# Scores with the keys in the partitions, maxima from a pass of their own, and a rotary turn in sums and differences

## The chip, the cores and the metric

The kernel runs on one core of a Trainium2 chip. The metric is device time in microseconds, the median of some runs. Beside the runs there is one profiled execution; its trace gives the durations used below. The engines are PE (matrix products, with PEld for loading weights), DVE, ACT and POOL (elementwise work), and SP, which here only issues DMAs.

## What is computed

A transformer block on x with 2048 rows and 1024 columns, all in float32:

```
h  = layernorm(x)
q, k, v = h Wq, h Wk, h Wv          # 16 heads of 64
q, k = rotary(q), rotary(k)         # t*cos + swapped(t)*sin, neighbours (0,1), (2,3), ... swapped, no sign
a  = softmax(mask(q k^T) / 8) v     # causal
x  = x + layernorm(a Wo)
x  = x + layernorm((silu(g Wg) * (g Wu)) Wd)   # g = layernorm(x); Wg, Wu, Wd from 4-bit codes and scales
```

## The kernel before

**Precision.** A float32 value is kept as a high part (rounded to the matmul's type fp32r) and a low part, the rest. A product of two such values is three matmuls (`mm3`, lines 225 to 227: high x high, high x low, low x high). ACT writes the high part, and DVE (or POOL) subtracts it for the low part.

**Stages.** Rows of x are normalized and transposed (`plan_rows`); q, k and v are projected for pairs of heads m and column groups c of 512 rows (`plan_qkv`), and written to DRAM as high and low parts (qs, ks, vs). Attention works in 64 blocks (head h, group J of 512 query rows). Then the attention rows are projected with Wo and normalized (five of the sixteen row tiles in `plan_project`, the other eleven in `attended`, `project`, `residual`), and the feed-forward part follows (gate and up for 22 column tiles, then a down projection in seven products).

**The order of the work.** All of the first part, until the end of attention and the first five row tiles, is written down as steps: an engine, a cost in microseconds, what it comes after, which buffers (`Room`) it takes, and a place `at` at which it is wanted. `Plan.order` replays the steps greedily: at each point it takes the step that could start first by these costs, the earlier place first among equals, on five in-order engines with limited buffers. The instructions are issued in that order. A chunk's values are wanted `LATE = 5` places after the scores of its block; a block (h, J) takes 4J + 4 places, and the 64 blocks 640. Loads are wanted `AHEAD = 8` places before. What follows the last query load in the program (the eleven row tiles, the feed-forward part) is ordered by a scheduler of the framework.

**A block of attention.** `plan_scores` makes scores with the queries in the partitions: for each of four tiles of 128 queries and each group of up to 512 keys, two matmuls into a bank S (line 322), DVE's maximum with the mask added on the diagonal (327, 329), and ACT's exponential with a running sum (334). When two query tiles are done, small operations on DVE and ACT (362 to 384) combine maxima and sums, and POOL scales each tile of probabilities by its factor (395). `plan_weighted` then takes chunks of 128 keys: PE transposes up to four 128 x 128 tiles of probabilities into a bank T (411), ACT and DVE split them into two parts (419, 422), and two matmuls with V add to a bank O (414). V holds its high and low parts side by side, 128 columns; at the end ACT copies one half and DVE adds the other (430, 431), and one DMA stores the block's result (attd). Matmuls on the diagonal are 512, 384, 256 and 128 wide. In all there are 640 score tiles, 640 chunks and 2176 transposes.

**Rotary.** After its projection, a tile of q or k is copied by ACT out of its bank (580), DVE makes a copy with neighbours swapped (612) and multiplies by the cosines (613), POOL multiplies the swapped copy by the sines and adds (614, 615), and ACT and DVE split the sum (616, 620).

**Buffers.** SBUF is cut into slots by size: 7 "hd" and 6 "pa" of 8 KB per partition, 4 "w", 4 "xc", 5 "f4" of 4 KB, 3 "pw", 4 "t2" of 2 KB and so on. The eight PSUM banks are F (1, projections), S (3, scores), T (3, transposes) and O (1).

Of the kernel before, what the change touches and what calls it, by code (L numbers as in the profile page):

```python
# [33 lines left out]
LATE = 5  # L34
# [6 lines left out]
EXPS = {512: 0.68, 384: 0.57, 256: 0.46, 128: 0.36}  # L41
CASTS = {512: 0.475, 384: 0.37, 256: 0.262, 128: 0.15}
PAIRED = {512: 0.602, 384: 0.468, 256: 0.334, 128: 0.202}
SCALES = {512: 0.668, 384: 0.562, 256: 0.45, 128: 0.347}
# [8 lines left out]
WO_AT = 26  # L53
PROJECT_AT = 36
PROJECT_STEP = 9
BATCH = 2
STEP = 4
FIRST = (0, 1, 2, 3)
# [18 lines left out]
class Room:  # L77
    def __init__(self, tag, make):
        self.tag, self.make, self.left, self.tile, self.open = tag, make, 0, None, False

# [14 lines left out]
class Plan:  # L95
# [4 lines left out]
    def add(self, engine, busy, lag, emit, after=(), rooms=(), at=0.0, port=False):  # L100
        step = Step(engine, busy, lag, emit, after, rooms, at, port)
        step.index = len(self.steps)
        self.steps.append(step)
        for a in step.after:
            a.next.append(step)
        for r in rooms:
            r.left += 1
        return step

    def order(self):  # L110
# [14 lines left out]
        while len(done) < len(self.steps):  # L125
            best = None
            for e, waiting in ready.items():
                for step in waiting:
                    t = max(step.ready, clock[e], wire - BACKLOG if e == "SP" else 0.0, port if step.port else 0.0)
                    for r in step.rooms:  # L130
                        if not r.open:
                            if queues[r.tag][-1] is not r or not self.free[r.tag]:
                                break
                            t = max(t, min(self.free[r.tag]))
                    else:
                        key = (t, step.at, step.index)
                        if best is None or key < best[0]:
                            best = key, step
# [3 lines left out]
            for r in step.rooms:  # L142
                if not r.open:
                    r.open = True
                    queues[r.tag].pop()
                    self.free[r.tag].remove(min(self.free[r.tag]))
# [9 lines left out]
            for r in step.rooms:  # L156
                r.left -= 1
                held[r] = max(held.get(r, 0.0), end + 0.05)
                if not r.left:
                    self.free[r.tag].append(held[r])  # L160
# [10 lines left out]
def block_kernel(ctx, tc, x, wq, wk, wv, wo, gu_codes, gu_scales, d_codes, d_scales, cos_sin, out):  # L171
# [12 lines left out]
    BANKS = {"F": 1, "S": 3, "T": 3, "O": 1}  # L184
    BANK_ORDER = ("F", "S", "S", "S", "T", "T", "T", "O")
# [21 lines left out]
    V.tensor_copy(mask_b, mask_f)  # L207
    nhalf = const.tile([P, 1], F32, name="nhalf")
# [68 lines left out]
    attd = [dram.tile([E, 512], F32, tag=f"at{c}", name=f"at{c}") for c in range(NC)]  # L277
# [11 lines left out]
    plan = Plan({"S": 3, "T": 3, "F": 1, "O": 1} | {t: SLOTS[t][0] for t in ("hd", "w", "xc", "pa", "pb", "f4", "pw", "t2", "ol")} | {"stats": 6, "ln": 6})  # L289
    kept, wrooms, xrooms, x_kept, shared, at_kept, wo_rooms = {}, {}, {}, {}, {}, {c: [] for c in range(NC)}, []  # L290

    def room(tag, shape, dtype, name):
        return Room(tag, lambda: slot(tag, shape, dtype, name))
# [10 lines left out]
    def plan_scores(J, q, half, k, q_in, k_in, start):  # L304
        nh = J + 1
        at = start
        prob = [room("pa", [P, 4, 512], F32, "prob") for _ in range(nh)]
        scaled, made = {}, {}
        stats = None
        for j in range(4):  # L310
            w = (4 * J + j + 1) * P
            if j % BATCH == 0:
                stats = Room("stats", lambda: [small.tile([P, BATCH, 4], F32, tag=n, name=n)[:, :, :nh] for n in ("mxs", "sums")])
            for i in range(nh):
# [4 lines left out]
                def score(b=b, e=e, s=s, j=j):  # L319
                    o = s()[:, : e - b]  # L320
                    for a in range(2):
                        T.matmul(o, lhsT=q()[:, half, a, j * P : (j + 1) * P], rhs=k()[:, b:e], start=a == 0, stop=a == 1)  # L322

                def top(b=b, e=e, s=s, j=j, i=i, diag=e == w, stats=stats):
                    o, mx = s()[:, : e - b], stats()[0][:, j % BATCH, i : i + 1]
# [5 lines left out]
                def power(b=b, e=e, s=s, j=j, i=i, diag=e == w, stats=stats):  # L331
                    mxs, sums = stats()
                    mx = mxs[:, j % BATCH, i : i + 1]
                    A.activation(  # L334
                        prob[i]()[:, j, : e - b],
                        s()[:, : e - b],
                        AF.Exp,
                        bias=mx,
                        scale=-1.0 if diag else 1.0,
                        accum_out=sums[:, j % BATCH, i : i + 1],  # L340
                    )

                x = on("PE", 2 * ROW[n], score, [q_in, k_in[i]], (s, q, k), at)
                y = on("DVE", PAIRED[n], top, [x], (s, stats), at, 0.055 if e == w else 0.0)
                z = on("ACT", EXPS[n], power, [y], (s, stats, prob[i]), at)
                made[j, i] = y, z
            if j % BATCH < BATCH - 1:
                continue
            rows = range(j - BATCH + 1, j + 1)
            tops = [made[jj, i][0] for jj in rows for i in range(nh)]  # L350
            sums_in = [made[jj, i][1] for jj in rows for i in range(nh)]
            got = {}

            def little(n, shape, got=got):
                got[n] = small.tile(shape, F32, tag=n, name=n)
                return got[n]

            if nh == 1:

                def invert(stats=stats, little=little, got=got):  # L360
                    got["rc"] = little("rc", [P, BATCH, 4])[:, :, :1]
                    V.reciprocal(got["rc"], stats()[1])

                last = on("DVE", 0.075, invert, sums_in, (stats,), at)
            else:

                def spread(stats=stats, little=little, got=got):
                    mxs = stats()[0]
                    nm = little("nm", [P, BATCH, 1])
                    V.tensor_reduce(nm, mxs, AX.X, ALU.min)  # L370
                    got["cf"] = little("cf", [P, BATCH, 4])[:, :, :nh]
                    V.tensor_tensor(got["cf"], mxs, nm.to_broadcast([P, BATCH, nh]), ALU.subtract)

                def weigh(got=got):
                    A.activation(got["cf"], got["cf"], AF.Exp, scale=-1.0)

                def total(stats=stats, little=little, got=got):
                    sums, cf = stats()[1], got["cf"]
                    sm = little("sm", [P, BATCH, 1])
                    V.tensor_tensor(sums, sums, cf, ALU.mult)  # L380
                    V.tensor_reduce(sm, sums, AX.X, ALU.add)
                    V.reciprocal(sm, sm)
                    got["rc"] = little("rc", [P, BATCH, 4])[:, :, :nh]
                    V.tensor_tensor(got["rc"], cf, sm.to_broadcast([P, BATCH, nh]), ALU.mult)  # L384

                first = on("DVE", 0.276, spread, tops, (stats,), at, port=True)
                second = on("ACT", 0.1, weigh, [first], (stats,), at)
                last = on("DVE", 0.671, total, [second] + sums_in, (stats,), at, port=True)
            for i in range(nh):
                for jj in rows:  # L390
                    n = min(512, (4 * J + jj + 1) * P - i * 512)

                    def scale(i=i, jj=jj, n=n, got=got):
                        p = prob[i]()[:, jj, :n]
                        G.tensor_scalar(p, p, got["rc"][:, jj % BATCH, i : i + 1], 0.0, ALU.mult, ALU.add)  # L395

                    scaled[i, jj] = on("POOL", SCALES[n], scale, [last, made[jj, i][1]], (prob[i], stats), at)
        return prob, scaled

    def plan_weighted(h, J, prob, scaled, v, v_in, start, pace):  # L400
        o, nk, chain = bank_room("O", "o"), 4 * J + 4, None
        for kb in range(nk):
# [3 lines left out]
            at = start + LATE + kb * pace  # L406
            pt, pw, pr = bank_room("T", "pt"), room("pw", [P, 2, 512], FR, "pw"), prob[kb // 4]

            def turned(kb=kb, j0=j0, pt=pt, pr=pr):
                for j in range(j0, 4):  # L410
                    T.transpose(pt()[:, j * P : (j + 1) * P], pr()[:, j, kb % 4 * P : (kb % 4 + 1) * P], ident)  # L411

            def times(a, kb=kb, cs=cs, pw=pw):
                T.matmul(  # L414
                    o()[:, cs], lhsT=v()[:, kb, :], rhs=pw()[:, a, cs], start=kb == 0 and a == 0, stop=kb == nk - 1 and a == 1
                )

            def rounded(cs=cs, pw=pw, pt=pt):
                A.copy(pw()[:, 0, cs], pt()[:, cs])  # L419

            def rest(cs=cs, pw=pw, pt=pt):
                V.tensor_tensor(pw()[:, 1, cs], pt()[:, cs], f32(pw()[:, 0, cs]), ALU.subtract)  # L422

            x = on("PE", (4 - j0) * TURN, turned, [scaled[kb // 4, j] for j in range(j0, 4)], (pt, pr), at)
# [727 lines left out]
```

## Time and profile before

| what | value |
|---|---|
| median of three runs | 2930.93 us (2929.71 to 2931.02) |
| profiled execution | 2933.72 us |
| its span, first to last instruction | 2931.9 us |
| granted clock of PE | 0.998 |
| PE, DVE, ACT, POOL busy | 99%, 70%, 58%, 33% of the span |
| DMA | 534.96 MB, 182 GB/s in the mean |

The page gives, for the profiled execution: busy times; the span in 40 slices with the busy tenths of each engine; DMA queues; the chain of work that ended last, followed back from the end; groups of instructions by source line, with their count, busy time, mean duration and the idle time of the engine before them; DMA issues with their time to landing. The trace behind it answers for single lines, tiles or stretches of time. In the trace, attention's first scores (line 322) start in the stretch from 75 to 150 us, and its last products with V (line 414) end in that from 1425 to 1500 us.

| stretch, us | PE busy, us | DVE | ACT | POOL | DMA share |
|---|---|---|---|---|---|
| 225 to 300 | 74.91 | 59.53 | 53.32 | 27.86 | 0.60 |
| 1050 to 1125 | 73.16 | 64.98 | 58.96 | 32.44 | 0.51 |
| 1275 to 1350 | 71.63 | 51.92 | 54.61 | 43.75 | 0.55 |
| 1500 to 1575 | 75.00 | 42.13 | 39.49 | 21.82 | 0.59 |
| 1800 to 1875 | 75.00 | 59.12 | 46.77 | 22.00 | 0.46 |

### The profile page before, as it was taken

Reading aid. Unit: us, or ns where it says so; the run is one execution under the profiler, and the core shown is the slowest. Engines: PE = TensorE matmul, PEld = TensorE weight load, DVE = VectorE, ACT = ScalarE, POOL = GpSimd, SP = SyncE. Lnnn points to the kernel's source line nnn. Section 1 sums busy time; section 2 is a strip of 40 time slices with the busy share of each in tenths; the row PEclk is TensorE's granted clock in tenths of the full one; section 3 lists DMA queues with packets and bytes.
Section 4 is the critical chain, followed back from the end, with each engine's and each line's share of the span. In section 5 each row is a group of like instructions: output and inputs, shape, how many; then the busy total and the mean of one; then the engine's idle time right before and its main releaser. Section 6 shows DMA issues by size and latency. Waiting matters only on the chain.

```text
span 2931.9 us, 42504 instructions
## 1 busy us (share of the span) xinstructions
PE 2888.4 (99%) x14192; PEld 2396.7 (82%) x14192; DVE 2050.5 (70%) x4167; ACT 1696.6 (58%) x3573; POOL 963.1 (33%) x1055
## 2 busy tenths in 40 slices
PE   8999999999999999999999999999999999999998
PEld 7878888888888888878787888888888888888887
DVE  7577887887878788777666766668766668443347
ACT  5366776676767677775556555556545546422234
POOL 5343444444434443554331221223222124000034
PEclk9999999999999999999999999999999999999999
DMA  9785676764858548573465443444443446644446
GB/s 325 270 243 207 186 224 216 234 195 151 256 181 223 201 138 262 168 229 117 148 219 169 149 136 118 137 137 155 136 136 120 133 137 204 233 141 150 147 140 226
DMA packets 271196, 534.96 MB, mean 182 GB/s; under 512 B 22912, under 2 KB 113024, under 8 KB 255104
## 3 DMA queue, kind: packets, MB, share of 16 engines
q1 hardware_dynamic: 270976, 532.24, 56.8%
q8 instruction: 112, 1.84, 0.3%
q14 instruction: 108, 0.88, 0.1%
HBM read 370.93 MB, written 161.22 MB: 182 GB/s over the span
## 4 chain that ended last, share of the span: by engine, by line
PE 91%; DVE 2%; ACT 2%; DMA 2%; issue 1%; POOL 1%; SPq 1%; POOLq 0%; DVEq 0%; ACTq 0%
PE bk L226 14%; PE bk L227 14%; PE bk L225 14%; PE o L414 8%; PE s L322 8%; PE pt L411 7%; PE qkv L225 6%; PE qkv L227 6%; PE qkv L226 6%; PE pj L658 2%; PE pj L789 1%; PE pj L787 1%; PE pj L788 1%; ACT prob L334 1%; PE pt L515 1%
## 5 line engine op out<-in xcount | busy, mean ns | idle before, releaser
L395 POOL TENSOR_SCALAR prob<-prob,rc 128x512 f32<-128x512 f32 (+3 forms) x640 | 398.9, 646 | 517.9 <-DVE rc L384 350.9
L225 PE MATMUL bk<-x,wt 128*128 128x512 f32 x1376 | 534.0, 390 | 0.8 <-ACT x L231 0.5
L227 PE MATMUL bk<-x,wt 128*128 128x512 f32 x1376 | 534.3, 390 | 0.0
L226 PE MATMUL bk<-x,wt 128*128 128x512 f32 x1376 | 534.2, 390 | 0.0
L334 ACT ACTIVATE prob<-s,mxs 128x512 f32<-128x512 f32 (+3 forms) x640 | 402.6, 631 | 146.1 <-DVE mxs L329 87.0
L422 DVE TENSOR_TENSOR pw<-pt,pw 128x512 fp32r<-128x512 f32 (+3 forms) x640 | 377.3, 605 | 96.9 <-ACT pw L419 91.9
L419 ACT CAST pw<-pt 128x512 fp32r<-128x512 f32 (+3 forms) x640 | 325.9, 528 | 159.8 <-PE pt L411 147.8
L846 ACT ACTIVATE ln<-cs,bias 128x512 f32<-128x512 f32 x520 | 354.5, 718 | 94.2 <-DVE cs L839 28.2
L414 PE MATMUL o<-pw,v 128*128 128x512 f32 (+3 forms) x1280 | 402.6, 381 | 5.4 <-ACT pw L419 3.0
L322 PE MATMUL s<-k,q 128*128 128x512 f32 (+3 forms) x1280 | 368.8, 380 | 8.0 <-ACT prob L334 6.2
L411 PE MATMUL pt<-ident,prob 128*128 128x128 f32 x2176 | 325.8, 273 | 1.8 <-DVE pw L422 1.8
L411 PEld LDWEIGHTS pt<-ident,prob 128*128 128x128 f32 x2176 | 264.3, 140 | 54.8 <-DVE pw L422 3.4
L225 PEld LDWEIGHTS bk<-x,wt 128*128 128x128 f32 x1376 | 258.5, 188 | 55.1 <-ACT x L231 0.8
L227 PEld LDWEIGHTS bk<-x,wt 128*128 128x128 f32 x1376 | 258.7, 188 | 54.1 <-DVE wt L232 0.3
L226 PEld LDWEIGHTS bk<-x,wt 128*128 128x128 f32 x1376 | 258.8, 188 | 53.5
L329 DVE TENSOR_REDUCE mxs<-s 128x1 f32<-128x512 f32 x384 | 262.1, 684 | 53.8 <-PE s L322 51.8
L414 PEld LDWEIGHTS o<-pw,v 128*128 128x128 f32 x1280 | 231.2, 189 | 57.7 <-DVE pw L422 11.1
L322 PEld LDWEIGHTS s<-k,q 128*128 128x128 f32 x1280 | 215.6, 189 | 45.0 <-ACT prob L334 17.7
L226 PE MATMUL bk<-bt,at 128*128 128x512 f32 x616 | 239.6, 389 | 0.0
L227 PE MATMUL bk<-bt,at 128*128 128x512 f32 x616 | 238.8, 389 | 0.0
L225 PE MATMUL bk<-bt,at 128*128 128x512 f32 x616 | 238.7, 389 | 0.0
L225 PE MATMUL qkv<-xc,w 128*128 128x512 f32 x576 | 236.9, 411 | 0.2 <-PE pt L411 0.2
(159 smaller groups left out, 4995.0 us busy)
## 6 DMA issues: line engine op xcount, KB each, us to landing
xc<-xd SPq DMA_DIRECT2D x96, 1024.0 KB, 6.9
q<-qs SPq DMA_DIRECT2D x128, 256.0 KB, 7.0
ast<-S SPq DMA_DIRECT2D x44, 512.0 KB, 3.6
cs<-in_gu_scales SPq DMA_DIRECT2D x172, 128.0 KB, 3.3
cs<-in_gu_codes SPq DMA_DIRECT2D x86, 256.0 KB, 3.1
A<-in SPq DMA_DIRECT2D x66, 256.0 KB, 2.3
S<-in SPq DMA_DIRECT2D x66, 256.0 KB, 2.6
ast<-A SPq DMA_DIRECT2D x33, 512.0 KB, 4.5
```

What stands on the lines that cost most here:

```text
L225: r = T.matmul(o, lhsT=w[:, 0], rhs=xx[:, 0], start=first, stop=False)
L226: T.matmul(o, lhsT=w[:, 0], rhs=xx[:, 1], start=False, stop=False)
L227: T.matmul(o, lhsT=w[:, 1], rhs=xx[:, 0], start=False, stop=last)
L322: T.matmul(o, lhsT=q()[:, half, a, j * P : (j + 1) * P], rhs=k()[:, b:e], start=a == 0, stop=a == 1)
L329: V.tensor_reduce(mx, o, AX.X, ALU.max, negate=True)
L334: A.activation(prob[i]()[:, j, : e - b], s()[:, : e - b], AF.Exp, bias=mx, scale=-1.0 if diag else 1.0, accum_out=sums[:, j % BATCH, i : i ...
L395: G.tensor_scalar(p, p, got["rc"][:, jj % BATCH, i : i + 1], 0.0, ALU.mult, ALU.add)
L411: T.transpose(pt()[:, j * P : (j + 1) * P], pr()[:, j, kb % 4 * P : (kb % 4 + 1) * P], ident)
L414: T.matmul(o()[:, cs], lhsT=v()[:, kb, :], rhs=pw()[:, a, cs], start=kb == 0 and a == 0, stop=kb == nk - 1 and a == 1)
L419: A.copy(pw()[:, 0, cs], pt()[:, cs])
L422: V.tensor_tensor(pw()[:, 1, cs], pt()[:, cs], f32(pw()[:, 0, cs]), ALU.subtract)
L846: A.activation(ln, c8, AF.Prelu, bias=bias_of[ab], scale=ab[0], alpha=ab[2])
```

## The change

**Attention.** `plan_scores` and `plan_weighted` give way to `plan_tops` and `plan_values`. A first pass makes rough scores, with the high part of q alone (one matmul instead of two), in the old form with queries in the partitions, and DVE takes the negated maximum of each query row. A DMA writes these 512 values to DRAM, and another reads them back as one row of the tile that holds q's low part. The second pass makes scores with the keys in the partitions, 128 keys by up to 512 queries: one matmul of k (both parts) with q's high part, one with a tile k2 (k's high part and a row of ones) and q's low part with the row of negated maxima, so that the sum arrives less its maximum; on the diagonal a third, bf16, adds the mask. ACT takes the exponential twice, once into SBUF rounded to fp32r (the high part), once in place in PSUM; DVE subtracts for the low part. Nothing is transposed, and the probabilities aren't scaled.

The products with V go to two banks: V's tile holds low part, high part and 64 columns of ones; the high part of the probabilities is multiplied by the first 128 columns into O, the low part by the last 128 into U, which so also gets the sums of the low parts. The sums of the high parts are added up by POOL over a block's chunks, split by ACT and DVE, and added to U by two matmuls with ones. At the block's end ACT copies O and U, and four DMAs store three partial results and the row of sums.

```diff
+                def rough(b=b, e=e, s=s, j=j):
+                    T.matmul(s()[:, : e - b], lhsT=q()[:, half, 0, j * P : (j + 1) * P], rhs=k()[:, b:e], start=True, stop=True)
...
+        x = fetch(lambda: tops[h][J].rearrange("j p -> p j"), lambda: f32(stats()[1]), 0.01, [x], (stats,), at, WRITE)
+        return fetch(lambda: f32(q()[D : D + 1, half, 1, :]), lambda: tops[h][J : J + 1].rearrange("o j p -> o (j p)"), 0.01, [x], (q,), at, READ)
...
+            def score(s=s, cs=cs, ks_=ks_, diag=kb >= 4 * J):
+                T.matmul(s()[:, cs], lhsT=k()[:, ks_], rhs=q()[:, half, 0, cs], start=True, stop=False)
+                if diag:
+                    T.matmul(s()[:, cs.start : cs.start + P], lhsT=mask_b[:, 384:], rhs=ident_b, start=False, stop=False)
+                T.matmul(s()[:, cs], lhsT=k2()[: D + 1, ks_], rhs=q()[: D + 1, half, 1, cs], start=False, stop=True)
...
+                A.activation(pw()[:, 0, cs], s()[:, cs], AF.Exp)
...
+                A.activation(s()[:, cs], s()[:, cs], AF.Exp)
...
+                V.tensor_tensor(pw()[:, 1, cs], s()[:, cs], f32(pw()[:, 0, cs]), ALU.subtract)
...
+                T.matmul(
+                    (o, u)[a]()[:, cs], lhsT=piece()[:, kb % 8, a * D : a * D + P], rhs=pw()[:, a, cs], start=kb == 0, stop=kb == nk - 1 and a == 0
                 )
...
+            def added(kb=kb, cs=cs, pw=pw, prev=summed[:1]):
+                G.tensor_tensor(acc()[:, cs], f32(prev[0]()[:, 0, cs]) if kb == 1 and J else acc()[:, cs], f32(pw()[:, 0, cs]), ALU.add)
...
+            T.matmul(u(), lhsT=low_ones, rhs=ah[a](), start=False, stop=a == 1)
```

**Output projection.** A row tile's input is now the sum of three stored parts times the reciprocal of the sums (`plan_factors` makes the reciprocals once for each J and stores them; they are read back repeated over the 64 rows of a head). The same stands in `plan_project` and in `attended`:

```diff
+        load(af, part_of(J, 0, cs))
+        for n in range(2):
+            load(f32(a2[n]), part_of(J, n + 1, cs))
+            V.tensor_tensor(af, af, f32(a2[n]), ALU.add)
+        for r in range(2):
+            load(sums[r * D : (r + 1) * D], sums_of(J, r, cs))
+        V.tensor_tensor(af, af, sums, ALU.mult)
         split(*a2, af)
```

**Rotary.** In `plan_w`, DVE turns neighbouring columns of Wq and Wk into their sum and their difference (two passes over 512 elements per partition for each weight tile), and Wq's factor is 1/16 rather than 1/8. In sums and differences the rotary turn is one multiplication by a table of cos + sin and cos - sin, half as large as the two tables before. DVE multiplies straight out of the bank; ACT's copy, DVE's swap and POOL's two operations go.

```diff
-                y = on("DVE", 0.64, lambda t1=t1, sh=sh: V.stream_shuffle(sh(), t1(), [i ^ 1 for i in range(32)]), [x], (t1, sh), p)
-                z = on("DVE", 0.61, lambda t1=t1: V.tensor_tensor(t1(), t1(), tab()[:, 0, :], ALU.mult), [y, tabbed], (t1, tab), p, port=True)
-                g = on("POOL", 1.29, lambda sh=sh: G.tensor_tensor(sh(), sh(), tab()[:, 1, :], ALU.mult), [y, tabbed], (sh, tab), p)
-                g = on("POOL", 1.29, lambda t1=t1, sh=sh: G.tensor_tensor(t1(), t1(), sh(), ALU.add), [g, z], (sh, t1), p)
+                x = on("DVE", 0.602, lambda t1=t1, f=f: V.tensor_tensor(t1(), f(), tab(), ALU.mult), [chain, tabbed], (f, t1, tab), p)
```

**The plan.** Values are wanted 20 places after their scores; places of the output projection and of Wo's loads move; some buffers get a limit of their own within a slot size. V and k2 hold six "pa" slots through all of attention (two heads each). PSUM is F 1, S 2, T 3, O 1, U 1.

```diff
-LATE = 5
+LATE = 20
+LAST_LATE = 20
...
-WO_AT = 26
+WO_AT = 22
 PROJECT_AT = 36
-PROJECT_STEP = 9
+PROJECT_STEP = 6
...
-    BANKS = {"F": 1, "S": 3, "T": 3, "O": 1}
+    BANKS = {"F": 1, "S": 2, "T": 3, "O": 1, "U": 1}
```

## The prediction

> **What bounds the kernel now.** I read the page's busy shares and slices first, then its chain of work that ended last, then groups, the order of time on PE, and stretches.
>
> ```profile
> span 2931.9 us, 42504 instructions
> PE 2888.4 (99%) x14192; PEld 2396.7 (82%) x14192; DVE 2050.5 (70%) x4167; ACT 1696.6 (58%) x3573; POOL 963.1 (33%) x1055
> ...
> PE   8999999999999999999999999999999999999998
> ...
> PE 91%; DVE 2%; ACT 2%; DMA 2%; issue 1%; POOL 1%; SPq 1%; POOLq 0%; DVEq 0%; ACTq 0%
> PE bk L226 14%; PE bk L227 14%; PE bk L225 14%; PE o L414 8%; PE s L322 8%; PE pt L411 7%; PE qkv L225 6%; PE qkv L227 6%; PE qkv L226 6%; PE pj L658 2%; PE pj L789 1%; PE pj L787 1%; PE pj L788 1%; ACT prob L334 1%; PE pt L515 1%
> ```
>
> PE is busy in every slice and holds 91% of the chain; the other engines have room. So the change is worth what it takes from PE's own path, unless another resource becomes late. The chain prices the three steps that change: scores (s) 8%, transposes (pt) 7%, products with V (o) 8%; one per cent is 29.3 us. A group's busy time is no price here: pipelined matmuls overlap, so starts have to be compared.
>
> ```profile
> 1329.81 5.73 PE L658 MATMUL pj<-wo,a 128*128 128x512 f32 x24
> 1335.38 0.62 PE L414 MATMUL o<-pw,v 128*128 128x512 f32 x2
> 1335.83 0.61 PE L322 MATMUL s<-k,q 128*128 128x512 f32 x2
> ...
> 1343.40 1.47 PE L411 MATMUL pt<-ident,prob 128*128 128x128 f32 x12
> 1344.68 0.50 PE L414 MATMUL o<-pw,v 128*128 128x512 f32 x1
> ```
>
> Two 512-column products take 1335.83 - 1335.38 = 0.45 us, 0.225 each; twelve transposes take 1.28 us, 0.107 each. The page agrees: 7% of the span is 205 us over 2176 transposes, 0.094 each.
>
> ```profile
> L395 POOL TENSOR_SCALAR prob<-prob,rc 128x512 f32<-128x512 f32 (+3 forms) x640 | 398.9, 646 | 517.9 <-DVE rc L384 350.9
> L334 ACT ACTIVATE prob<-s,mxs 128x512 f32<-128x512 f32 (+3 forms) x640 | 402.6, 631 | 146.1 <-DVE mxs L329 87.0
> L422 DVE TENSOR_TENSOR pw<-pt,pw 128x512 fp32r<-128x512 f32 (+3 forms) x640 | 377.3, 605 | 96.9 <-ACT pw L419 91.9
> L419 ACT CAST pw<-pt 128x512 fp32r<-128x512 f32 (+3 forms) x640 | 325.9, 528 | 159.8 <-PE pt L411 147.8
> L322 PE MATMUL s<-k,q 128*128 128x512 f32 (+3 forms) x1280 | 368.8, 380 | 8.0 <-ACT prob L334 6.2
> L411 PE MATMUL pt<-ident,prob 128*128 128x128 f32 x2176 | 325.8, 273 | 1.8 <-DVE pw L422 1.8
> ```
>
> The counts to take from these are 640 score tiles, 640 chunks of values, 2176 transposes.
>
> ```profile
> 150.00:1425.00 1275.00, 1259.96 (x6847) 1047.41 (x6847) 1005.89 (x2510) 888.75 (x2291) 558.25 (x752) 1.00 0.65 201
> ...
> 1400.00:1575.00 175.00, 172.73 (x853) 143.61 (x852) 111.45 (x244) 99.30 (x168) 54.50 (x52) 1.00 0.58 192
> ```
>
> The first stretch is attention beside the projections of q, k and v: PE 99%, DVE 79%, ACT 70%, POOL 44%, DMA 0.65. The second is the output projection of the eleven row tiles that the plan doesn't hold: DVE 64%, DMA share 0.58 at 192 GB/s.
>
> **PE's path in attention.** Removed: 2176 transposes, 205 us by the chain (0.088 to 0.107 each gives 191 to 233). Added: the pass for the maxima, 640 matmuls, half of the old score row of 1280: half of 8%, 117 us (110 to 125 by the rounding). The transposed scores are again 1280 matmuls of the old widths, the products with V stay 1280. Sixteen diagonal masks in each of 16 heads, 256 bf16 matmuls of 128 columns: no row shows one; a quarter of the 512-column time is 0.056, a transpose 0.107; I take 0.085, from two 128-column products (o, at 1327.43 us) whose successor starts 0.17 us after the first: 22 us (14 to 27). Two totals for each of 64 blocks: 128 x 0.225 = 29 us. Sum: -205 + 117 + 22 + 29 = **-37 us** (-80 to -10 by the ends).
>
> The Trainium skill, "TensorE: Matmul & The Clock Gate", Part 4, gives about 275 ns for a transpose in a kernel's context. By it the removal would be 598 us and the sum of this part -430; the rows above, with starts 0.107 us apart, decide.
>
> **Hand-overs.** In a chain restricted to 225 to 1275 us, PE holds 93%; the other 7%, 74 us, are waits for ACT, DVE, SP and loads. A chunk keeps four hand-overs (s, pt, o, o become maxima, st, o, u), and values now trail scores by 20 places of the plan rather than 5. Score banks fall from three to two, but each is free after DVE's maximum rather than after ACT's exponential. At the end of a block the one U bank waits for POOL's last add (1.29), ACT's and DVE's split (0.59, 0.69), two totals (0.45) and ACT's copy (0.59): 3.6 us, beside which PE has the next block's scores and five chunk buffers. I take no difference; from both sides, 4% or 12% in place of 7%, over 1050 us: -32 to +53 us.
>
> **The other engines in attention.** ACT: each exponential (0.696 at 512 columns, and 0.202 for reading its sum) and each cast (0.593) become two plain exponentials; ACT writing PSUM appears in no row, so 0.593 to 0.696 each. 402.6 + 129.4 (the reads) + 325.9 = 858 us fall to between 652 and 805, twice the one row or the other; three block copies of 0.59 in 64 blocks add 113. Off the path, as ACT is idle for 30% of the stretch. DVE loses 108 us of small statistics and the rotary shuffle and a multiplication (0.746, 0.948, against one of about 0.69: 64 us), and gains 32 passes over weights (22 us) and the additions below; it falls from 79%. POOL loses 399 us of scaling and 170 us of rotary, and gains 576 adds: 384 x 1.29 plus 64 x 1.29 x 1.5 for the narrow ones is 620 us; off the path at about half of the stretch, and with 620 / 640 = 0.97 us a chunk against PE's 1275 / 622 = 2.05 (1245 of the 1280 o matmuls lie in the stretch, two a chunk). If that cover were gone, a chunk could go no faster than 1.29.
>
> In the rotary rows the DVE product of two SBUF tiles beside POOL's takes 0.948 us, a like one without POOL 0.704. The skill's "SBUF — State Buffer", Who interferes with whom, speaks against this change: a DVE instruction with two SBUF inputs and a reading GpSimd one exclude each other for the whole instruction. By it the 64 new splits could wait an add each, 83 us of DVE; by the row, 16 us; either lies in DVE's idle fifth.
>
> **Queues.** Each block issues five more DMAs on SP: the maxima out and back, two more partial results and a row of sums; loads for k2 come on top, while q's second half and the rotary table shrink. The store of maxima writes single words; no row shows such a store. By the nearest rows a small store lands in 4.7 us (at, 128 KB) and a load in 5.3 to 10.1, so the round trip is 10 to 20 us; behind it SP holds the next loads, for which the plan leaves eight places ahead, and the values' 20 places are about 44 us (640 places in some 1400 us). I take 0, up to 15 if SP stops behind the store.
>
> **The output projection.** Each row tile now loads three partial tiles of 0.5 MB and 0.5 MB of factors rather than 0.5 MB, and has three more DVE operations of 128 x 1024; the subtraction of that shape here has a median of 1.226 us. For eleven tiles: 33 x 1.226 = 40 us on DVE, 151 of 175 us; 16.5 MB at 192 / 0.58 = 331 GB/s is 50 us of DMA, also 151 of 175. Both are near 87%, so the cover is thin: I take 12 us (a quarter of the dearer one), bounds 0 and 50. The five planned tiles have 18 us more on DVE beside attention: in its idle fifth.
>
> **Start.** Two DVE passes of about 0.7 us now stand between the first weights' landing and their split. First qkv starts at 15.95 us; the first rows' transposes occupy PE before it. I take 1 us (0 to 2).
>
> **Sum**: -37 + 12 + 1 = -24. The profiled execution took 2933.7 (span 2931.9 and 1.8 around it); it becomes 2910, and the median, 2.8 lower (2930.9), becomes **2907**.
>
> **Rivals.** (a) Longer lag pays: hand-overs fall to 4%: -32 more, 2875. For it: PE always finds other ready work; against: the chain inside a chunk is as long as ever. (b) A wash: PE's removed time was partly cover for ACT and DVE; half of the 37 stays and the projection costs 20: 2907 + 18 + 8 = 2933. (c) Slower by the projection: loads become the bound of that stage, from the point where their share passes 0.93, the highest whole-stretch share in this trace (the first 75 us). Price 50 us instead of 12: 2907 + 38 = 2945. For it: 87% by my sum, factors and partial tiles in 512-byte rows; against: the tiles are fetched ahead. (d) Slower by hand-overs: 12%, +53: 2960.
>
> **Numbers.** Forecast 0.40 (own range 2890 to 2924), (a) 0.10, (b) 0.15, (c) 0.20, (d) 0.15. Faster by over 0.2%, about what a measurement of this kernel can tell, is below 2925: 0.50; within it 0.15; slower 0.35. The range takes in (a) and stops just short of (d), which leaves out no more than its 0.15: 2872 to 2958.
>
> **What would show it.** pt L411 gone from the chain, the maxima's matmuls at about 4%, total PE chain of attention down by 37 us; PE full in attention; idle PE, if any, between the end of attention and the first gate and up products, with waits on the adds or their loads. Wrong: the share of waits in attention's chain far from 7%, POOL's adds far above 1.29 us, SP waiting for the maxima's store.

## The result, and the profile after

The changed kernel takes **3124.18 us** in the median of four runs (3120.86 to 3131.5), against 2930.77 for the kernel before on the same chip: 1.0659 times as long (95% interval 1.0646 to 1.0672). It is 193 us slower; the prediction was 24 us faster, range 2872 to 2958. The forecast is wrong in its sign, and the range missed too.

The page of the changed kernel's profile: busy shares, then two rows of the 40 slices (tenths), then the chain.

```profile
span 3119.8 us, 39830 instructions
...
PE 2932.3 (94%) x13040; PEld 2350.8 (75%) x13040; DVE 2013.8 (65%) x3581; ACT 1599.6 (51%) x2923; POOL 1044.0 (33%) x866
...
PE   8989899898998998978887999999999999999998
...
PEclk9999999999998999978998999999999999999999
...
PE 76%; DMA 14%; DVE 3%; ACT 3%; issue 2%; POOL 1%; SPq 1%; POOLq 0%; ACTq 0%; DVEq 0%
```

No engine has become the bound: DVE and ACT are less busy than before. PE has holes in the first 22 slices (attention and the output projection), none in the feed-forward part, and the chain of waits now spends 14% in DMA, where it spent 2%. In time: the last product with V ends at 1564 us (before 1448), the first gate and up product starts at 1740 (before 1552). So attention is 116 us longer and the stage behind it 72 us (176 for 104); the feed-forward part takes about 1369 us in both. Some of the 72 is work that moved: of the 768 products of the output projection, 336 were issued ahead of attention's last product before the change and 216 after it, and 120 products at 0.225 us are 27 us.

The DMA queue's own waits (engine, line, what it waited for: us in total, times, longest) and, below, pieces of the chain of waits in order of time:

```profile
SPq L317 <- DMA mx<-nm: 287.7, 54, 12.6
```

```profile
592.36 11.83 DMA mx<-nm
604.29 8.48 DMA q<-mx
614.69 11.29 DMA at<-wide
```

The wait for the maxima's store holds SP longer than any other wait does. But the third piece has nothing to do with the maxima: a plain store of results, 128 KB, takes 11.29 us where it took 4.7 before. The same is seen in the packets. Between 150 and 1400 us the kernel before has 2 packets that take over 2 us; the changed one has 549, 127 of them over 4 us. And in a stretch in which both move some 200 GB/s, the DMA engines' share goes from 0.66 to 0.82. First before, then after (PE, PEld, DVE, ACT, POOL busy; granted clock, DMA share, GB/s):

```profile
150.00:1400.00 1250.00, 1236.33 (x6729) 1028.01 (x6729) 990.98 (x2481) 876.74 (x2269) 547.65 (x739) 1.00 0.66 202
```

```profile
150.00:1400.00 1250.00, 1147.36 (x5183) 891.43 (x5181) 829.41 (x1723) 715.87 (x1510) 593.53 (x521) 0.95 0.82 202
...
1350.00:1425.00 75.00, 50.16 (x170) 34.51 (x169) 39.78 (x92) 27.36 (x57) 28.33 (x22) 0.70 0.68 128
```

The last row is the worst stretch: PE busy for 50 of 75 us, and at a granted clock of 0.70, so that part of what work is left runs slowly as well. In the trace the clock is either full or half, and in this row it is half for 44 of the 75 us, in pieces that are multiples of 3.41 us. The Trainium skill, "TensorE: Matmul & The Clock Gate", Part 1, says that PE falls to half its clock after an idle window of some 3.4 us and needs one busy window to return. The two levels and the length of the pieces agree with it, and in the whole run PE was busy for at least 3.0 us of the 3.41 ahead of each return; but the 3.41 us ahead of a fall were not always idle: PE was busy for up to 2.4 of them.

### The profile page after: what moved, and what is told of

The parts are those of the page before. It is cut to its first block, busy times and chain, and to the rows that moved or that the text cites. A ratio compares the mean times of both kernels' runs of the same rounds, so it can differ in the third digit from the quotient of the medians.

```text
span 3119.8 us, 39830 instructions
## 1 busy us (share of the span) xinstructions
PE 2932.3 (94%) x13040; PEld 2350.8 (75%) x13040; DVE 2013.8 (65%) x3581; ACT 1599.6 (51%) x2923; POOL 1044.0 (33%) x866
## 4 chain that ended last, share of the span: by engine, by line
PE 76%; DMA 14%; DVE 3%; ACT 3%; issue 2%; POOL 1%; SPq 1%; POOLq 0%; ACTq 0%; DVEq 0%
PE bk L240 14%; PE bk L241 14%; PE bk L242 14%; PE qkv L240 5%; PE qkv L241 5%; PE qkv L242 5%; PE st L373 3%; PE u L385 3%; PE o L385 3%; PE st L370 3%; PE s L334 3%; DMA mx<-nm 2%; DMA at<-wide 2%; DMA xc<-xd 2%; PE pj L663 1%
## 5 line engine op out<-in xcount | busy, mean ns | idle before, releaser
L390 POOL TENSOR_TENSOR wide<-wide,pw 128x512 f32<-128x512 f32 (+3 forms) x321 | 372.5, 1161 | 374.2 <-ACT pw L376 279.4
L379 ACT ACTIVATE st<-st 128x512 f32<-128x512 f32 (+3 forms) x640 | 332.4, 531 | 0.0
L376 ACT ACTIVATE pw<-st 128x512 fp32r<-128x512 f32 (+3 forms) x384 | 206.2, 548 | 196.8 <-PE st L373 181.2
L382 DVE TENSOR_TENSOR pw<-st,pw 128x512 fp32r<-128x512 f32 (+3 forms) x384 | 235.2, 622 | 107.4 <-ACT st L379 97.9
L240 PE MATMUL qkv<-xc,w 128*128 128x512 f32 x624 | 255.6, 410 | 21.5 <-DMA xc<-xd 20.6
L390 POOL TENSOR_TENSOR wide<-wide,pair 128x512 f32<-128x512 f32 (+2 forms) x207 | 217.1, 1049 | 173.9 <-ACT pair L376 164.1
L373 PE MATMUL st<-q,k 65*128 65x512 f32 (+3 forms) x640 | 260.7, 408 | 8.0 <-DMA q<-mx 8.0
L334 PE MATMUL s<-k,q 128*128 128x512 f32 (+3 forms) x640 | 236.3, 389 | 31.3 <-DVE mxs L339 13.5
L370 PE MATMUL st<-q,k 128*128 128x512 f32 (+3 forms) x640 | 244.0, 381 | 18.2 <-DVE pw L382 12.8
L241 PE MATMUL qkv<-xc,w 128*128 128x512 f32 x624 | 250.1, 401 | 0.0
L242 PE MATMUL qkv<-xc,w 128*128 128x512 f32 x624 | 249.2, 399 | 0.0
```

The source lines that it names most:

```text
L240: r = T.matmul(o, lhsT=w[:, 0], rhs=xx[:, 0], start=first, stop=False)
L241: T.matmul(o, lhsT=w[:, 0], rhs=xx[:, 1], start=False, stop=False)
L242: T.matmul(o, lhsT=w[:, 1], rhs=xx[:, 0], start=False, stop=last)
L334: T.matmul(s()[:, : e - b], lhsT=q()[:, half, 0, j * P : (j + 1) * P], rhs=k()[:, b:e], start=True, stop=True)
L370: T.matmul(s()[:, cs], lhsT=k()[:, ks_], rhs=q()[:, half, 0, cs], start=True, stop=False)
L373: T.matmul(s()[:, cs], lhsT=k2()[: D + 1, ks_], rhs=q()[: D + 1, half, 1, cs], start=False, stop=True)
```

## The experiments

The theories. **T1**: the store of the maxima in single words (512 pieces of 4 bytes) costs attention its 116 us, either because SP stands in order behind it (T1a) or because it slows all other transfers (T1b). **T2**: the added loads and DVE operations cost the projection 72 us. **Rival R**: attention's own hand-overs (banks, lag, the chain behind the maxima) cost it, whatever the DMAs do.

### The store

**e1_contig**: 128 runs of 16 bytes instead of 512 words, read back in that order.

```diff
-    tops = [dram.tile([NC, 4, P], F32, ...
+    tops = [dram.tile([NC, P, 4], F32, ...
-        x = fetch(lambda: tops[h][J].rearrange("j p -> p j"), ...
+        x = fetch(lambda: tops[h][J], ...
```

> The maxima of a block are stored as 128 runs of 16 bytes rather than 512 single words, and read back in that order. A query is then shifted by the maximum of another query of its block, which the division by the sums takes out again. Theory T1, the store of single words holds up the DMA queues and costs attention its 116 us, in the form that the price goes with the number of pieces: a quarter of the pieces, so some 85 us come back and the time is 3030 to 3050. T1 in the form that any store in pieces far below 512 bytes costs a fixed 8 us or so of standing queues: 3105 to 3125. Rival R, attention is slower by its own hand-overs (two S banks, the one U bank, the chain behind the maxima) and not by DMA: 3115 to 3130.

**e2_nowait** loads the row from a buffer of zeros, so that nothing waits for the store; **e3_nostore** drops the store as well.

```diff
-lambda: tops[h][J : J + 1].rearrange("o j p -> o (j p)")
+lambda: zero_d
```

> The maxima are stored as in the changed kernel, but the row that is read back comes from a buffer of zeros filled at the start, so no load waits for the store (left out: the shift by the maximum). T1a, SP stands in order behind the load that waits for the store: 3010 to 3040, the top wait of SP on nm gone. T1b, the store itself keeps the DMA engines from other work for 8 us or so, 64 times: 3080 to 3125 with DMA still at 0.75 to 0.9 of its time in attention. Rival R (hand-overs of the chunks): 3110 to 3130.

> As the run that reads zeros, and the maxima are not stored either (left out: the shift by the maximum). T1 in either form: the 116 us of attention come back, 3000 to 3020, the granted clock returns to 0.99 and the DMA share in attention to about 0.65; if the shorter PE path that was forecast then shows as well, down to 2970. Rival R: within 15 us of 3124.

Measured: e1 2997.21 us (1.0224, 1.0207 to 1.0241), e2 3105.52 (1.0593, 1.0573 to 1.0613), e3 2999.46 (1.0232, 1.0217 to 1.0247). Rival R falls as the main cause: without the store 125 us are gone, and in e1 and e3 the last product with V ends at 1437 us instead of 1564. T1a is worth 3124 - 3106 = 19 us, T1b 3106 - 2999 = 106. And 128 runs of 16 bytes cost nothing that can be measured (2997 against 2999); my price by the number of pieces, which gave 3030 to 3050, was wrong. The stretches above, in e1: more bytes in less DMA time, and the worst 75 us recover most of their work.

```profile
150.00:1400.00 1250.00, 1220.55 (x5603) 946.87 (x5602) 915.55 (x1874) 782.07 (x1642) 661.67 (x576) 0.98 0.71 215
...
1350.00:1425.00 75.00, 66.78 (x273) 48.35 (x271) 48.37 (x81) 46.71 (x86) 46.44 (x38) 0.95 0.74 215
```

**e11_before_words**: the store alone, put into the kernel before, once for each block; nothing reads it.

```diff
+        fetch(lambda: words_d[h][J].rearrange("j p -> p j"), lambda: words, 0.01, [y], (), at, WRITE)
```

> The kernel before, with one more DMA at the end of each of the 64 blocks: a tile of 128 x 4 constants stored as 512 single words, which nothing reads and nothing waits for. Theory T1b, the scattered store by itself slows the transfers beside it: 2990 to 3060, with packets of over 2 us in numbers (549 of them in the changed kernel's attention, 2 in the kernel before). Rival: it is harmless where loads have more lead, as the kernel before has no load behind it: 2930 to 2945.

Measured: 3034.27 us (1.0352, 1.0339 to 1.0366), 103 us slower, with 626 packets of over 2 us. That is the price of the store without any part of the new attention, and it agrees with the 106 above. The chain of waits in this kernel, in order of time:

```profile
302.95 15.64 DMA at<-ol
335.12 20.90 DMA ks<-hl
356.09 9.33 DMA wf<-in_wq
```

None of the three is the store of words: the chain waits for ordinary stores and loads, and between 150 and 1400 us the DMA share is again 0.82, at 193 GB/s. Of the 626 slow packets, 3 are packets of 4 bytes and the others hold 512 bytes or more. Most packets take as long as before (for 8 KB the median is 0.309 us in both kernels); what has grown is the tail: the slowest 1% of the 8 KB packets take over 3.42 us, where they took over 1.04. What in the store does it? **e17_words_apart** puts the 512 words 64 bytes apart, **e18_words_128** stores 128 neighbouring words.

```diff
-        fetch(lambda: words_d[h][J].rearrange("j p -> p j"), lambda: words, ...
+        fetch(lambda: words_d[h][J, :, :, 0].rearrange("j p -> p j"), lambda: words, ...      # e17, words_d [NC, 4, P, 16]
+        fetch(lambda: words_d[h][J, 0:1].rearrange("j p -> p j"), lambda: words[:, 0:1], ...  # e18
```

> The kernel before with 64 stores of 512 single words that nothing reads, as in the run that gave 3034, but each word 64 bytes from the next. If the price is that of 512 pieces: 3015 to 3050. If it comes from words that are neighbours in DRAM and are written at once: 2930 to 2950.

> The same with 128 neighbouring words in place of 512, one of each partition. If the price goes by pieces: a quarter of 103, 2950 to 2965. If 128 pieces are free whatever their size, as 128 runs of 16 bytes were: 2930 to 2938. If neighbours are what counts, about a quarter as well, or more if the few lines are contended more: 2950 to 3000.

Measured: e17 2934.61 us (1.0015, 1.0006 to 1.0025), 10 packets of over 2 us; e18 2994.22 (1.0221, 1.0203 to 1.0240), 745 packets. So it is neither the number of pieces nor their size alone: 512 single words apart cost 5 us, 128 that are neighbours cost 64. The store's own landing (issue to landing, smallest, median, largest), in e11 and in e17:

```profile
DMA to landing us min/median/max: 8.0/11.1/19.1
```

```profile
DMA to landing us min/median/max: 2.2/4.5/9.7
```

The 4.5 us is about what the prediction had taken for a small store (4.7). What it didn't know is that neighbouring words, here each from another partition, more than double it and stretch what runs beside it.

### The projection

**e4_plain_projection** (on the changed kernel) and **e13_contig_plain** (on e1) load the first part alone, without factors, and so leave out two partial results and the division; **e7_loads_only** (on e1) loads everything but leaves out the two additions and the multiplication, **e8_no_factors** (on e1) leaves out the factors and the multiplication.

```diff
-        for n in range(2):
-            load(f32(a2[n]), part_of(J, n + 1, cs))
-            V.tensor_tensor(af, af, f32(a2[n]), ALU.add)
-        for r in range(2):
-            load(sums[r * D : (r + 1) * D], sums_of(J, r, cs))
-        V.tensor_tensor(af, af, sums, ALU.mult)
```

> The row tiles of the output projection load only the first of the three partial results, and no factors (left out: two partial results and the division by the sums). Theory T2, the stage from the last product of attention to the first gate and up product costs 72 us more because of the four more loads and three more DVE operations of a tile: 3050 to 3065, attention unchanged at about 1564 us for its last product. Rival: the stage is late for what attention leaves undone (planned tiles pushed back, Wo's loads), and the loads matter little: 3095 to 3125.

> The 16-byte store; a row tile loads its three parts and the factors, but the two additions and the multiplication on DVE are left out (the product takes the first part alone). Theory D, the 70 us of the projection are DVE's three more passes of 128 x 1024 for a tile: 2930 to 2950. Theory L, they are the four more loads, DVE matters little: 2980 to 2997.

> The 16-byte store; a row tile loads and adds its three parts, but neither loads the factors nor multiplies (the division is left out). If the factor loads, 512-byte rows repeated over 64 partitions, are the dear part of theory L: 2940 to 2960. If the price goes by bytes (a quarter of the added volume) or by DVE operations (one of three): 2970 to 2985.

> The 16-byte store and row tiles that load the first part alone, without factors (left out: two partial results and the division). If the two costs add and are all of it: 2997 - 70 = 2927, attention no more than 11 us shorter than before, of which 5 are the rotary edit's. If the forecast path of PE (37 us less) shows once loads are on time: 2890 to 2905.

Measured: e4 3047.97 us (1.0396, 1.0379 to 1.0414), e7 2971.58 (1.0138, 1.0124 to 1.0152), e8 2970.28 (1.0133, 1.0119 to 1.0146), e13 2938.07 (1.0022, 1.0012 to 1.0032). The stage takes 106 us again in e4 (1557 to 1663) and in e13 (1448 to 1554), about as before the change (104), and 335 of the products are again issued ahead of it. Its price is 76 us on the changed kernel and 59 on e1; on e1, the DVE operations are worth 26 and the factors with their multiplication 27, so it is neither loads nor DVE alone. The stage's length by itself is no price: in e8 it is back at 110 us, with 336 products ahead of it, but attention ends at 1471, 34 us later than in e1. e4 ended 2 us below its range, e13 11 us above the 2927, and e7 between its two ranges. The chain of the changed kernel in this stage shows how:

```profile
1584.42 8.22 DMA sums<-inv
...
1594.98 6.32 DMA af<-at
1606.79 2.51 DVE a L247
```

A tile's input is a line of loads of 6 to 8 us and DVE operations, fetched only one tile ahead, whereas PE needs 48 x 0.225 = 10.8 us for a tile. By the products behind attention's last one, a tile takes 15.4 us in e1 (552 products in 177 us) and 11.7 in e13. That the depth of one tile is what makes the line too long is read from the chain; no run fetched further ahead. In the stretch from 1450 to 1610 us of e1 the DMA share is 0.79 and DVE is busy for 70%: neither is full, and still PE is busy for 133 of 160 us at clock 0.89. In e13 PE is busy without a gap:

```profile
1450.00:1610.00 160.00, 133.47 (x577) 108.25 (x576) 111.66 (x198) 69.48 (x106) 40.71 (x32) 0.89 0.79 232
```

```profile
1455.00:1550.00 95.00, 95.00 (x447) 79.09 (x446) 59.48 (x139) 57.57 (x91) 31.64 (x25) 1.00 0.62 213
```

### Making up for both

Three kernels try to keep the new scores and a light projection, all with the 16-byte store. **e5_contig_divided** divides at the block's end, **e9_pool_divided** has POOL do it, **e12_combined** adds there and leaves the factors to the projection.

```diff
+        x = on("DVE", ..., V.tensor_tensor(oo()[:D], o()[:D], oo()[:D], ALU.add), ...
+        x = on("DVE", ..., V.tensor_tensor(oo()[:D], u()[:D], oo()[:D], ALU.add), ...
+        y = on("DVE", ..., V.reciprocal(uo()[:D], uo()[:D]), ...                  # e5; e9: G.tensor_tensor(..., minus, ALU.pow); e12: none
+        x = on("DVE", ..., V.tensor_tensor(oo()[:D], oo()[:D], uo()[:D], ALU.mult), ...  # e9: on POOL; e12: none
```

> Maxima stored in 16-byte runs as before; at a block's end DVE adds the halves of O and U, takes the reciprocal of the sums and multiplies, and one DMA stores the finished rows, so that the row tiles of the projection load one part and no factors, as in the kernel before. Nothing is left out. Theory: both costs of the change are gone, 997 for the store and 70 us of the projection, and what is left of attention's gain (11 us in the run with 16-byte runs) shows: 2997 - 70 = 2927, range 2915 to 2935. Rival: the longer block end (six more small operations on DVE in each of 64 blocks before U is free) costs a us in each block: 2980 to 3000. The figure 997 stands for the 127 us found between the two ways of storing.

> As the run that divides at the block's end, but the reciprocal (a power of -1) and the multiplication are made by POOL; DVE keeps two additions of 64 x 512 a block. Nothing is left out. Theory H: there the reciprocal of 3.33 us stood in DVE's queue ahead of the maxima and the remainders of the next block, and PE lost some 4 us in each of 64 blocks. Then without it the block end is cheap and the projection's 70 us are saved: 2925 to 2950, if POOL's power of 64 x 512 stays below some 3 us. Rival: the block end is dear because O and U come free later, wherever the division is made: 3050 or more.

> The 16-byte store; DVE adds the halves of O and U at the block's end and one part is stored, so that a row tile of the projection loads one part and the factors, and only multiplies. Nothing is left out. By the parts of the projection's price (70 us, of which 27 for factors and multiplication): 2997 - 43 = 2954, range 2945 to 2965. If two DVE additions at the block's end (1.35 us) delay PE as the reciprocal did, some 1.2 us for each of DVE's: 3040 to 3060.

Measured: e5 3187.06 us (1.0873, 1.0858 to 1.0887), e9 7911.53 (2.6986, 2.6954 to 2.7018), e12 3018.94 (1.0298, 1.0285 to 1.0311). e5 and e12 lie in none of their ranges; e9 is above its range for a gain, and what it decides is said below. In e5 the projection is light (106 us from the last product with V to the first gate and up product), but attention is 263 us longer than in e1; 27 of them are 120 projection products that e1 makes later, and the rest is 3.7 us for each block. DVE's order of time at one block's end (start, duration):

```profile
705.46 0.67 DVE L422 TENSOR_TENSOR wide<-u,wide 64x512 f32<-64x512 f32 x1
706.06 3.33 DVE L423 RECIPROCAL wide<-wide 64x512 f32<-64x512 f32 x1
709.32 0.62 DVE L341 TENSOR_REDUCE mxs<-s 128x1 f32<-128x512 f32 x1
```

The reciprocal takes 3.33 us, five times a sum of the same shape, and the maximum behind it starts only when it is done; DVE is busy for 71% of the span. PE's waits in e5 (engine, line, what it waited for: us in total, times, longest) tell the queue from the banks O and U that come free later:

```profile
PE s L334 <- DVE mxs L341: 53.2, 35, 3.5
...
PE s L334 <- DVE mxs L339: 22.6, 20, 2.8
...
PE u L385 <- DVE wide L422: 11.2, 7, 2.3
```

With a further 6.7 us for O (line 420), PE waits 76 us for maxima and 18 for the banks; in e1 it waits 9 us for maxima. So the queue is the larger part of what can be named, but these waits don't add up to the whole loss.

The Trainium skill's "VectorE: DVE Perf Modes", Walkthrough, says that the reciprocal is an iterated division with a repeat count of 8, and gives no price; here it is 6.5 ns for each element of a partition. e9 can't decide theory H (the queue): POOL's power takes 82 us for the same shape (for one column of 128 rows it takes 0.55 us in the kernel before), so the kernel measures that alone.

```profile
L425 POOL TENSOR_TENSOR wide<-wide,minus x64: 81917/81921/82141, 171.5 to 6352.3; 64x512 f32<-64x512 f32 x64
```

e12 answers in its place: two additions for a block, 1.35 us of DVE, make attention 37 us longer than in e1 (1473 against 1437), of which 6 are 25 projection products that e1 makes later, and the stage behind it is only 18 us shorter. The work that was moved out of the block's end, and made the projection heavy, was not free there either.

### Lag, banks, rotary

> The 16-byte store, and the values trail their scores by 5 places of the plan, as in the kernel before, instead of 20. If the longer lag covers the trip of the maxima through DRAM (store and load, 8 to 12 us): 3010 to 3060. If it does nothing: 2992 to 3000. If it only lengthens the stretch behind the last scores, in which PE has little else to do: 2975 to 2990.

> The 16-byte store; the lag of the values shrinks from 20 places to 8 over the last 160 places of attention. If the shortfall lies behind the last scores, where PE has only the trailing values and planned row tiles: 2980 to 2990. If the lag is needed there as elsewhere (5 places throughout cost 77 us): 3005 to 3030.

> The 16-byte store; the values trail by 32 places, by 20 at the end as before. If waits for the maxima's trip still cost time at 20: 2975 to 2990. If 20 covers it: 2994 to 3005.

> The 16-byte store; two U banks and two T banks rather than one and three. If the end of a block, where the next block's second products wait for the one U bank, costs attention its shortfall: 2970 to 2985. If it does not, and transposed scores need their three banks: 3000 to 3050.

> The kernel before with the rotary edit alone (weights in sums and differences, one table, one multiplication out of the bank); scores, maxima and projection as before. By the prediction's terms the removed ACT, DVE and POOL work lies beside PE: 2929 to 2934, the first qkv product 0 to 2 us later. Rival: the shorter way from a projection to its store (no ACT copy, no shuffle, no two POOL operations, 5 us) lets q, k and v arrive sooner, and the 11 us that attention gained come from here: 2915 to 2925.

Edits: `LATE = LAST_LATE = 5`; `LAST_LATE = 8`; `LATE = 32`; `BANKS` with T 2 and U 2; and in the kernel before, the rotary diff of the change. Measured: e10 3074.07 us (1.0486, 1.0472 to 1.0499), e14 3014.36 (1.0285, 1.0271 to 1.0299), e15 3036.55 (1.0359, 1.0345 to 1.0373), e16 3056.77 (1.0431, 1.0416 to 1.0445), e6 2925.93 (0.9983, 0.9974 to 0.9992). Against e1's 2997 the lag of 20 places is worth 77 us over 5, and both a longer one and a shorter end are worse; one T bank less and one U bank more costs 60 us. e10 and e16 ended 14 and 7 us above the ranges that came nearest. With lag 5 the trip of the maxima stands in the chain of waits even with the 16-byte store:

```profile
752.14 5.87 DMA q<-mx
...
915.54 8.93 DMA mx<-nm
```

e15 is 32 us above its highest range; why a lag of 32 is worse was not tried further. The rotary edit alone makes the kernel before 4.8 us faster (0.08% to 0.26%), just short of the range for a gain. It is the only version here that beats both kernels, by about as much as the measurement can tell.

## Why the prediction was wrong

The loss splits, one step after the other, into 127 us for the way the maxima are stored (3124 to 2997), 59 for the projection on top of it (2997 to 2938), and 6 that are left (2938 against 2932). For the last figure I add, in the traces, the time from each matmul's start to the next one's, by line; of each, at most 0.25 us counts as work, the rest as waiting.

| attention, us | before | e13 |
|---|---|---|
| scores, second pass (before: all scores) | 266 | 130 + 145, masks 10 |
| pass for the maxima | | 133 |
| transposes | 200 | |
| products with V | 266 | 132 + 130 |
| totals | | 31 |
| work | 732 | 711 |
| waiting | 48 | 81 |

- **PE's path** (forecast -37, ends -80 and -10): -21. Transposes -205 was -200; what PE's path pays is the distance from one start to the next, 0.092 us, and not the length of a transpose, 273 ns in the mean by its row, near the 275 that the prediction set aside. Scores and products with V, taken as unchanged, came out 10 us lower together. The maxima's pass is 133, not 117: the chain's 8% put less down to the scores than their 266 us from start to start, of which 133 is half. Totals 29 was 31. Masks 22 was about 25, in another place than thought: the mask itself takes 0.04 us, and the product after it is slower, for 145 us are spent in that line and 130 in its twin. Where no mask stands ahead of it, at 512 columns off the diagonal, both lines take 0.233 us. The timeline shows one at 128 columns: the mask starts at 588.05, the next product at 588.08, and what follows it 0.15 us later, where 128 columns took 0.07.

```profile
587.98 0.22 PE L370 MATMUL st<-q,k 128*128 128x128 f32 x1
588.05 0.23 PE L372 MATMUL st<-ident_b,mask_b 128*128 128x128 bf16 x1
588.08 0.31 PE L373 MATMUL st<-q,k 65*128 65x128 f32 x1
588.23 0.45 PE L334 MATMUL s<-k,q 128*128 128x512 f32 x1
```

- **Hand-overs** (forecast 0, bounds -32 to +53): +33, within the bounds. With the lag of 20 places they are dearer than before, and by e10's time and chain the lag is needed for the new trip through DRAM. So rival (a) is out, and (d) has the right sign and 33 of its 53 us.
- **Queues** (forecast 0, up to 15): **the step that failed.** I asked only how long SP stands behind the store and whether the lag covers the trip. That part was sized nearly rightly: 19 us (e2), a little over the bound of 15. What was missing is that a transfer of 2 KB can slow those beside it: 106 us (e2 to e3), and 103 without any of the new attention (e11). I had noted that no row shows such a store, and yet took its landing from a store of another form (128 KB in long rows) and left no upper bound for its effect on its neighbours.
- **The output projection** (forecast 12, bounds 0 to 50): 59 to 76, **a second step that failed**. The operations were sized rightly (median 1.225 us for 1.226), and the shares too high (70% and 0.79 in e1, for 87%). The model was wrong: it asked whether an engine's share reaches its end (rival (c) decided from 0.93), and neither did; by the chain, a tile's line of loads and operations became longer than PE's 10.8 us. Rival (c) named the right place, with 38 of the 47 us or more beyond the forecast, but not its condition.
- **Other engines**: POOL's 576 adds took 654 us for the 620 forecast. POOL is off the path, as said: it holds 1% of the chain of waits.
- **Start** (forecast 1, 0 to 2): the first product of q, k and v starts at 18.0 us for 16.0 before: 2.
- **Rotary**, costed at nothing beside PE: alone it gains 4.8 us, and the projections of q, k and v take 538 us rather than 546 by the count above (in e13; 544 with the rotary edit alone).

With the 127 and the 59 gone, the change would be worth nothing: -21 of work, +33 of waiting, -8 in the projections of q, k and v and +2 at the start make +6. The medians of e13 and the kernel before are 6 us apart, the spans of their two traces 4.4, so the account closes within some 2 us. This isn't a kernel that can be had, as e13 leaves out two partial results and the division. The figure is near rival (b), a wash, but by luck: that rival counted 20 us for the projection, which e13 doesn't pay.

## What to carry to other kernels

Look at a small DMA's layout before its size: here neighbouring single words of DRAM, each from another partition, slowed the transfers beside them, while 16-byte runs or words 64 bytes apart hardly did; where no row shows a form of transfer, bound what it does to the others too. Ask of a stage not only whether an engine is full, but also whether the line of loads and operations of one tile, at the depth to which it is fetched ahead, is shorter than PE's time for the tile. And work at a block's end can be dear on an engine that has room: on a DVE with a quarter of its time free, 1.35 us of additions a block made attention some 31 us longer over 64 blocks, and with a reciprocal of 3.33 us and a multiplication as well some 236.

## What was not expected of the hardware

- 64 stores of 2 KB in neighbouring single words cost 103 us, of 128 words (512 bytes) 64 us; the same 512 words 64 bytes apart 5 us (all in the kernel before); 128 runs of 16 bytes nothing that shows (in the changed kernel). The skill's "DMA: Bandwidth & Descriptors", Specifications, puts the line at 512 bytes, below which it says an engine reads, modifies and writes; in all four stores the pieces lie below it and only two are dear, so that line alone doesn't tell them apart. Whether two DMA engines that write to the same short stretch of DRAM are the cause, or whether it matters that the neighbours come from different partitions, was not tried; it stays open.
- A reciprocal of 64 x 512 on DVE takes 3.33 us, a power of the same shape on POOL 82 us.
- A bf16 matmul between fp32 ones takes 0.04 us, and the product behind it some 0.08 longer than its like (0.143 for 0.063 at 128 columns, 0.315 for 0.233 at 512).
